# Cross-attention with layer norm: the first transfers split over two queues, a shorter warm-up, and one tile squared before it is centred

## The chip, the cores and the metric

The kernel runs on one core of a Trainium2 chip. The metric is the device time of one execution in microseconds (us). Engines are named as in the profile: PE is TensorE, ACT is ScalarE, DVE is VectorE, POOL is GpSimd, SP is SyncE, which here only issues transfers. PEld is TensorE's loading of weights.

## The reference

Four batches of 2048 queries of width 512 attend to 77 context rows each, with 16 heads of width 32. A residual and a layer norm follow.

```python
qs = (q @ wq).reshape(Bq, Lq, H, HD).transpose(0, 2, 1, 3)
ks_ = (k @ wk).reshape(Bq, Lk, H, HD).transpose(0, 2, 1, 3)
vs = (v @ wv).reshape(Bq, Lk, H, HD).transpose(0, 2, 1, 3)
scores = jnp.einsum('bhqd,bhkd->bhqk', qs, ks_) / jnp.sqrt(jnp.float32(HD))
scores = jnp.where(mask[:, None, :, :], -jnp.inf, scores)
attn_w = jax.nn.softmax(scores, axis=-1)
attn = jnp.einsum('bhqk,bhkd->bhqd', attn_w, vs)
attn = attn.transpose(0, 2, 1, 3).reshape(Bq, Lq, H * HD)
out = attn @ wo + q
mu = jnp.mean(out, axis=-1, keepdims=True)
var = jnp.mean((out - mu) ** 2, axis=-1, keepdims=True)
return (out - mu) / jnp.sqrt(var + EPS) * gamma + beta
```

Here q is x (4 x 2048 x 512), k and v are both the context (4 x 77 x 512), all float32.

## The kernel before, in words

**Tiling.** The 8192 rows are 64 tiles of 128 rows; two tiles are a block, four are a group of 512 rows (`GRP`). A float32 product is made of three products in a rounded format (fp32r): each factor is split into a high part (a cast) and a low part (the rest), and high x high, low x high and high x low are summed. `split(hi, lo, src)` does the cast on ScalarE and the subtraction on VectorE. The width of 512 is cut into four chunks `c` of 128.

**The start.** GpSimd clears a small tile, and TensorE multiplies it by itself: `WARM` large products of 512 columns and then 18 small ones of 32. Their results are not used. Meanwhile the first 256 rows of x, already transposed (`xT0`, two transfers of two chunks each, into `xtf`), and the four chunks of `wq` (into `stage_a`) are loaded, 128 partitions of 2 KB per transfer. One of the six transfers is issued by ScalarE, the others by SP; behind them on SP stand the context (`ctx_f`), `wk`, the mask, the second 256 rows, `wv` and so on. For chunk 0, VectorE casts the weight (`wqh`), ScalarE the input (`xth`), VectorE then makes the low parts `xtl` and `wql`. The 48 products into the four banks `pq` (four chunks, three kinds, four column blocks) follow, and the 48 of the keys behind them (`pk`).

**What sets the order.** Each engine takes its own instructions in the order in which the code issues them. Waits between engines and transfers are set by a tool that follows the tiles. Transfers use eight counters in turn (`DMAHW0` to `DMAHW7`, "lanes" here): the ninth waits until the first has landed. An instruction carries one wait; where it needs more, further waits stand ahead of it as instructions of their own. ScalarE's load of its function table is put ahead of its first computing instruction.

**The middle and the end.** From tile 6 on the order is written out by hand as words in tables (`PAIR`, `JOINT`, `ORDER`): a letter is a step, the number its tile. For the end of the program the words that matter here are

- `I54` (`act_mean`) and `J54` (`act_squares`): ScalarE's mean of the rows of tile 54, and its sum of squares of (row - mean), both from the tile `od[54]`, named `o`;
- `y54` (`centre`): VectorE's (row - mean) x gamma, written back into the same tile;
- `u54` (`rsqrt_one`, GpSimd) and `z54` (`finish`, VectorE): the factor from the sum of squares, and the last step with it and beta;
- `h63.1` and `m63.1`: the reciprocals (VectorE) and the scaling (GpSimd) of the second half of tile 63's weights; `b30.1` and `b30.0`: the low part `AL` of block 30 on VectorE, after ScalarE's `AH`.

Of the kernel before, what the change touches and what calls it, by code (L numbers as in the profile page):

```python
# [17 lines left out]
P = 128  # L18
# [11 lines left out]
NC_D = D // P  # L30
# [2 lines left out]
MASKED = -3.0e38  # L33
CEIL = 2.9e38
EPS = 1.0e-5
WARM = 8
NPB = 3
KSCALE = 1.0 / HD**0.5
LATE = 48
# [19 lines left out]
P27.0s q63 u48 p48 T58.1 T58.2 P26.1s P27.1s P26.11s T58.3 e58.1 r57 t56 P27.11s n57 Q61 P27.6s f46 e58.2 T58.0 V26  # L59
q61 a26.1 t57 a26.0 x55 f48 e58.0 S59 P27.2s T59.2 P27.5s e58.3 T59.3 e59.3 P27.3s P28.4g P27.8s T59.0 O51 b26.0  # L60
P28.11g T59.1 P27.9s +51 P28.6g r58 e59.2 P28.5g O50 P27.10s b26.1 s51 e59.1 P27.4s n58 S60 Y0 u51 +50 P28.0s x57
e59.0 P28.7g P28.10s V27 T60.0 T60.1 a27.0 T60.2 a27.1 T60.3 e60.1 r59 t58 w46 P28.3s P28.9s S61 n59 O52 P28.1s
e60.3 b27.0 s50 T61.0 T61.3 t59 f49 u50 e61.0 e61.3 T61.2 b27.1 T61.1 O53 P28.8s P29.1g P29.9g e61.2 O54 S62 +52
e61.1 +53 s52 x54 r61 P28.2s V28 +54 P29.7g e60.2 x62 T62.1 T62.2 O55 p50 n61 e60.0 T62.3 x56 P29.4s r60 n60 T62.0
t61 v51 M0 P29.8s a28.0 a28.1 b28.1 b28.0 f50 t60 +55 O57 e62.2 P29.6s e62.1 P29.5s P29.10s +57 P30.6g P29.3s
P29.11s k51 P29.2s P29.0s P30.10s P30.1s e62.0 e62.3 u52 v52 S63 V29 P30.2s T63.0 P30.9s P30.5g s53 P30.7g P30.11a
s55 T63.1 r62 a29.1 P30.4s T63.3 P30.0s e63.0 P30.3s n62 b29.1 T63.2 O56 a29.0 b29.0 e63.1 I54 u53 e63.3 P30.8s s57
h63.0 y55 t62 +56 f51 O59 u55 e63.2 x58 O58 x60 k52 m63.0 y54 V30 h63.1 m63.1 I56 U62.7s U62.6s +59 J56 a30.1 u56
U62.4s U62.8s R63.0 U62.9s x61 U62.11s s59 y57 a30.0 u57 +58 u59 b30.1 b30.0 U62.5s z57 R63.1 y53 J54 R63.3 U62.1s
U62.0a R63.2 w48 E63.0a f52 w51 s58 U62.10s O60 U62.3s +60 w50 O61 U62.2a w52 y58 X63 M1 z53 E63.1a v56 v59 s60 z55  # L70
+61 y60 E63.2a u54 W62 u58 k56 E63.3a w49 w57 u60 z54 k59 c62 w54 I61 J61 W63 f56 z58 c63 d62 y61 w53 z60 w55 u61
f59 O62 w56 d63 z61 +62 s62 y62 w58 w61 w59 O63 u62 s63 z62 w60 y63 u63 w62 z63 w63
"""


# [1 line left out]
def xattn_layernorm(  # L77
# [15 lines left out]
    nc = tc.nc  # L93
# [10 lines left out]
    ring, kept, rows, summed = [], set(), {}, set()  # L104
    held = {}

    def bank(name):
        while len(ring) % 8 in kept:
            ring.append(ring[-8])
        ring.append(ring[-8] if kept else ps.tile([P, 512], F32, tag="mm", name=name))  # L110
        return ring[-1]
# [28 lines left out]
    stage_a = sb.tile([P, 2, NC_D, D], F32, tag="PT", name="stage_a")  # L140
# [9 lines left out]
    def wview(w, c):  # L150
        return w[c * P : (c + 1) * P, :]
# [522 lines left out]
    pw = bank("pw")  # L674
    for i in range(WARM):
        nc.tensor.matmul(pw, warm[:, :P], warm[:, None, :P].to_broadcast((P, 4, P)), start=True, stop=True)
    for i in range(18):
        nc.tensor.matmul(pw[:, :32], warm[:, :P], warm[:, :32], start=True, stop=True)

    for c in range(0, NC_D, 2):  # L680
# [2 lines left out]
    qd[0] = sb.tile([P, NG, GRP], F32, tag="q", name="q_0")  # L683
    x0h, x0l = (a[:, :, :BLK] for a in gx[0])
    f0 = {c: fx[0, c].rearrange("p c r -> p (c r)").rearrange("p (h c r) -> p h c r", h=2, c=2) for c in (0, 2)}
    for c in range(0, NC_D, 2):
        nc.sync.dma_start(f0[c][:, 0], xT0[0, :, c : c + 2])
        (nc.sync if c else nc.scalar).dma_start(stage_a[:, 0, c], wview(wq, c))
        nc.sync.dma_start(stage_a[:, 0, c + 1], wview(wq, c + 1))
    for c in range(NC_D):  # L690
        if c % 2 == 0:
            nc.sync.dma_start(ctx_f[:, c : c + 2], ctxT[:, c : c + 2])
# [312 lines left out]
```

## Time and profile before

| | us |
|---|---|
| median of three runs | 507.82 (507.53 to 508.34) |
| the profiled execution, its own time | 506.96 |
| its span in the profile | 505.2 |
| TensorE busy | 496.4 (98%) |
| ScalarE busy | 472.2 (93%) |
| VectorE busy | 463.3 (92%) |
| GpSimd busy | 427.0 (85%) |

The time of an execution is 1.76 us longer than the span, which runs from the first recorded instruction to the last. A row of the timeline has the start, the length, the engine, the line, the operation and what it writes and reads; neighbouring equal instructions are merged with their count, and products overlap, so the length of one is longer than the distance to the next. "SPq" and "ACTq" are the issuing of transfers by SP and ScalarE.

### The profile page before, as it was taken

How to read it: one execution, taken by the hardware profiler on the slowest of the kernel's cores; microseconds unless marked ns; L12 is line 12 of the kernel's file. 1: busy time of each engine (PE TensorE's matmuls, PEld its weight loads, DVE VectorE, ACT ScalarE, POOL GpSimd, SP SyncE). 2: the span in 40 equal slices, each digit the busy share in tenths (PEclk: the TensorE clock that was granted, in tenths of full speed). 3: DMA queues.
4: the chain of work that ended last, by engine and by line, in shares of the span. 5: the costliest groups of instructions: out<-in, count | busy, mean ns of one | idle time of the engine just before them, and what ended most of it. 6: DMA issues, size and time to landing. Idle time of an engine off the chain costs nothing.

```text
span 505.2 us, 20438 instructions
## 1 busy us (share of the span) xinstructions
PE 496.4 (98%) x6908; PEld 391.0 (77%) x6908; DVE 463.3 (92%) x2566; ACT 472.2 (93%) x2239; POOL 427.0 (85%) x384
## 2 busy tenths in 40 slices
PE   9999999999999999999999999999999999999994
PEld 7987778777777887777788777777877777777784
DVE  6698999999989998999999988999999889999997
ACT  6798999999999999999999999999999999999861
POOL 0659368989888998988999888889988888999994
PEclk9999999999999999999999999999999999999999
DMA  8945887677778779777878878787777878667665
GB/s 308 399 165 151 207 215 194 197 191 210 213 226 227 217 211 257 188 205 227 224 218 220 237 182 248 210 228 212 228 200 204 237 214 245 171 189 209 168 210 209
DMA packets 58280, 109.50 MB, mean 217 GB/s; under 512 B 9203, under 2 KB 10739, under 8 KB 58176
## 3 DMA queue, kind: packets, MB, share of 16 engines
q1 hardware_dynamic: 55776, 103.35, 72.5%
q0 software_dynamic: 1872, 4.20, 2.7%
q8 instruction: 55, 0.90, 0.8%
q10 hardware_dynamic: 528, 0.66, 0.4%
q14 instruction: 49, 0.40, 0.2%
HBM read 41.68 MB, written 16.78 MB: 116 GB/s over the span
## 4 chain that ended last, share of the span: by engine, by line
PE 90%; ACT 4%; DVE 3%; DMA 2%; issue 1%; SPq 1%; DVEq 0%; ACTq 0%
PE pq L192 31%; PE po L557 29%; PE pa L459 11%; PE sc L321 7%; PE sc L557 3%; ACT pbuf L379 3%; PE sc_e L321 2%; PE pv L258 2%; PE pk L218 1%; PE pq L709 1%; PE pq L190 1%; DMA PT<-B 1%; PE sc_f L321 1%; DMA xtf<-xT 1%; DVE pbuf L364 1%
## 5 line engine op out<-in xcount | busy, mean ns | idle before, releaser
L379 ACT ACTIVATE pbuf<-pbuf,nm 128x77 f32<-128x77 f32 x1024 | 352.5, 349 | 8.5 <-DVE nm L364 7.5
L379 ACT ACTIVATION_READ_ACCUMULATOR pbuf<-pbuf,nm 128x1 f32 x1024 | 193.5, 189 | 0.0
L390 POOL TENSOR_TENSOR pbuf<-pbuf,ri 128x1232 f32<-128x1232 f32 x63 | 145.9, 2317 | 19.7 <-DVE ri L385 15.7
L364 DVE CUSTOM_DVE_ANT_0 pbuf<-sc,mb 128x77 f32<-128x77 f32 x828 | 144.0, 232 | 5.9 <-PE sc L321 5.6
L192 PE MATMUL pq<-xtl,wqh 128*128 128x512 f32 (+1 forms) x256 | 98.3, 384 | 0.0
L192 PE MATMUL pq<-xth,wql 128*128 128x512 f32 (+1 forms) x256 | 98.2, 384 | 0.0
L413 DVE STREAM_TRANSPOSE B<-pbuf 128x1280 f32<-128x1280 f32 x63 | 94.6, 1503 | 0.4 <-POOL pbuf L390 0.2
L557 PE MATMUL po<-woh,AH 128*128 128x512 f32 x224 | 90.6, 405 | 0.0
L192 PE MATMUL pq<-xth,wqh 128*128 128x512 f32 (+1 forms) x230 | 88.6, 385 | 0.0
L557 PE MATMUL po<-wol,AH 128*128 128x512 f32 x224 | 87.4, 390 | 0.0
L585 POOL TENSOR_TENSOR o<-o,gam 128x512 f32<-128x512 f32 x53 | 68.7, 1297 | 21.0 <-ACT o L581 21.0
L557 PE MATMUL po<-woh,AL 128*128 128x512 f32 x224 | 86.5, 390 | 0.0
L364 DVE DVE_READ_ACCUMULATOR2_ANT nm<- 128x1 f32 x1024 | 84.7, 83 | 0.0
L586 POOL TENSOR_TENSOR o<-o,bet 128x512 f32<-128x512 f32 x53 | 68.4, 1290 | 4.2
L180 POOL TENSOR_TENSOR xtl<-xtf,xth 128x1024 fp32r<-128x1024 f32 x28 | 67.5, 2412 | 0.1
L459 PE MATMUL pa<-PT,vsb 96*32 96x256 f32 x960 | 58.2, 382 | 0.7 <-DMA PT<-B 0.3
L321 PE MATMUL sc<-kct,q 32*64 32x77 f32 x3312 | 55.2, 238 | 0.5 <-DVE q L209 0.5
L192 PEld LDWEIGHTS pq<-xth,wql 128*128 128x128 f32 x256 | 48.2, 188 | 8.4
L192 PEld LDWEIGHTS pq<-xtl,wqh 128*128 128x128 f32 x256 | 48.1, 188 | 8.5
L321 PEld LDWEIGHTS sc<-kct,q 32*64 32x64 f32 x3312 | 48.7, 130 | 6.5 <-issue 4.8
L557 PEld LDWEIGHTS po<-woh,AH 128*128 128x128 f32 x224 | 42.0, 188 | 10.8 <-DVE nm L364 0.4
L192 PEld LDWEIGHTS pq<-xth,wqh 128*128 128x128 f32 x230 | 43.2, 188 | 9.0
(176 smaller groups left out, 851.6 us busy)
## 6 DMA issues: line engine op xcount, KB each, us to landing
PT<-B SPq DMA_DIRECT2D x355, 128.0 KB
xtf<-xT SPq DMA_DIRECT2D x28, 512.0 KB
o<-x SPq DMA_DIRECT2D x56, 256.0 KB
out<-o SPq DMA_DIRECT2D x56, 256.0 KB
PT<-B POOLq DMA_DIRECT2D x16, 128.0 KB, 4.5
o_end<-x SPq DMA_DIRECT2D x7, 256.0 KB
out<-o_end SPq DMA_DIRECT2D x7, 256.0 KB
xtf<-xT SPq DMA_DIRECT2D x4, 256.0 KB
```

Source lines behind the costliest of these rows:

```text
L180: nc.gpsimd.tensor_tensor(l, fx.pop((g, c)), h.bitcast(F32), ALU.subtract)
L192: nc.tensor.matmul(pq, wc, r[:, c, rs], start=(n == 0), stop=(n == 11))
L258: nc.tensor.matmul(pv, ctx_s[c][i][:, r, :], v[c], start=(n == 0), stop=(n == 11))
L321: nc.tensor.matmul(scs[t][g, j][r0 : r0 + n], qd[t // 4][q, g, at : at + n], kct[q, g, t // TPB, keys_of(j)], start=True, stop=True,)
L364: nc.vector.tensor_tensor_reduce(pb[:, i // 2, (i % 2) * NK : (i % 2 + 1) * NK], scs[t][g, j], mb[:, t % TPB, keys_of(h)], -1.0, CEIL, ALU ...
L379: nc.scalar.activation(p, p, AF.Exp, bias=nmax[t][:, i : i + 1], scale=-1.0, accum_out=sums[t][:, i : i + 1])
L390: nc.gpsimd.tensor_tensor(pv, pv, rv.to_broadcast((P, NP, 2, NK)), ALU.mult)
L413: nc.vector.transpose(bt.rearrange("p c q r -> p q c r"), pbuf[t % NPB].rearrange("p q (c r) -> p q c r", c=5),)
L459: nc.tensor.matmul(pas[b, g // 2][HD * j : HD * (j + 1), (g % 2) * BLK : (g % 2 + 1) * BLK], vsb[:, 2 * b // TPB, HD * h : HD * (h + 1)], ...
L557: nc.tensor.matmul(pos[t][:, cols], a[:, c, rs], w[:, c, cols], start=go, stop=done)
L585: nc.gpsimd.tensor_tensor(o, o, gam, ALU.mult)
L586: nc.gpsimd.tensor_tensor(o, o, bet, ALU.add)
```

## The change

Four edits. Two of the eight large warm-up products go, and two small ones are added. The first transfer of x is cut into 96 and 32 partitions, both on SP, with half a chunk of `wq` between them. Chunk 0 of `wq` is cut into two halves of 64 partitions, one issued by ScalarE and one by SP; chunk 1 is cut into two halves too, both issued by ScalarE. And `y54` is moved in the table from ahead of `V30` to behind `J54`, so that the squares of tile 54 are taken from the rows themselves and not from the centred ones.

```diff
-WARM = 8
+WARM = 6
@@ ORDER (the rest of the table has the same words in the same order)
-... s57 h63.0 y55 t62 +56 f51 O59 u55 e63.2 x58 O58 x60 k52 m63.0 y54 V30 h63.1 m63.1 I56 ...
+... s57 h63.0 y55 t62 +56 f51 O59 u55 e63.2 x58 O58 x60 k52 m63.0 V30 h63.1 m63.1 I56 ...
-... b30.1 b30.0 U62.5s z57 R63.1 y53 J54 R63.3 U62.1s ...
+... b30.1 b30.0 U62.5s z57 R63.1 y53 J54 y54 R63.3 U62.1s ...
@@
-    for i in range(18):
+    for i in range(20):
         nc.tensor.matmul(pw[:, :32], warm[:, :P], warm[:, :32], start=True, stop=True)
@@
-    for c in range(0, NC_D, 2):
-        nc.sync.dma_start(f0[c][:, 0], xT0[0, :, c : c + 2])
-        (nc.sync if c else nc.scalar).dma_start(stage_a[:, 0, c], wview(wq, c))
-        nc.sync.dma_start(stage_a[:, 0, c + 1], wview(wq, c + 1))
+    def load_x0(queue, c, rows):
+        queue.dma_start(f0[c][rows, 0], xT0[0, rows, c : c + 2])
+
+    def load_wq(queue, c, rows):
+        queue.dma_start(stage_a[rows, 0, c], wview(wq, c)[rows])
+
+    first, second = slice(0, P // 2), slice(P // 2, P)
+    load_x0(nc.sync, 0, slice(0, 96))
+    load_wq(nc.scalar, 0, first)
+    load_wq(nc.sync, 0, second)
+    load_x0(nc.sync, 0, slice(96, P))
+    load_wq(nc.scalar, 1, first)
+    load_wq(nc.scalar, 1, second)
+    load_x0(nc.sync, 2, slice(0, P))
+    load_wq(nc.sync, 2, slice(0, P))
+    load_wq(nc.sync, 3, slice(0, P))
```

The order of the instructions, with the counters that each waits for. ScalarE's first instructions before:

```order
L688 DMA stage_a<-wq 128x512
L154 ACT_TABLE_LOAD
L154 CAST xth_129<-xtf_0_127 128x256 [waits DMAHW1_49]
L154 CAST xth_129<-xtf_0_127 128x256
L154 CAST wqh<-stage_a 128x512 [waits DMAHW2_49]
```

And now:

```order
L690 DMA stage_a<-wq 64x512 x3
L154 ACT_TABLE_LOAD [waits DMAHW5_49]
L154 CAST xth_129<-xtf_0_127 128x256 [waits DMAHW1_49]
L154 CAST xth_129<-xtf_0_127 128x256
L154 CAST wqh<-stage_a 128x512 [waits DMAHW4_49,DMAHW2_49]
```

ScalarE now issues three transfers instead of one; the first cast needs both pieces of x, and of its two waits the one for the piece of 32 partitions (DMAHW5) stands ahead of the table load.

SP's first transfers before:

```order
L687 DMA xtf_0_127<-xT 128x512
L689 DMA stage_a<-wq 128x512
L687 DMA xtf_2_128<-xT 128x512
L688 DMA stage_a<-wq 128x512
L689 DMA stage_a<-wq 128x512
L692 DMA ctx_f<-ctxT 128x768
L693 DMA stage_a<-wk 128x512
L693 DMA stage_a<-wk 128x512 [waits DMAHW0_49]
```

And now:

```order
L687 DMA xtf_0_127<-xT 96x512
L690 DMA stage_a<-wq 64x512
L687 DMA xtf_0_127<-xT 32x512
L687 DMA xtf_2_128<-xT 128x512
L690 DMA stage_a<-wq 128x512
L690 DMA stage_a<-wq 128x512 [waits DMAHW0_49]
L704 DMA ctx_f<-ctxT 128x768 [waits DMAHW1_49]
L705 DMA stage_a<-wk 128x512 [waits DMAHW2_49]
```

The second piece of x is third on SP, behind 64 rows of `wq`; and since the pieces use up the eight counters earlier, SP waits from its sixth transfer on instead of its eighth.

VectorE near the end, before (`o_54` is tile 54; `o_end` are the tiles from 56 on; the second row is `y54`, the third `h63.1`, the ninth and tenth `b30.1` and `b30.0`):

```order
L560 TENSOR_TENSOR o_end_7996<-sc_62_0_8488,o_end_7996 128x512
L655 SCALAR_TENSOR_TENSOR o_54_8534<-o_54_8534,mvt_54_8778,row_0_8609 128x512
L398 RECIPROCAL ri_63_8791<-sum_63_8668 128x8
L560 TENSOR_TENSOR o_end_7996<-sc_62_1_8489,o_end_7996 128x512
L595 BN_STATS st_59_8874<-o_end_7996 128x6
L601 BN_AGGR mvt_59_8876<-st_59_8874 128x2
L655 SCALAR_TENSOR_TENSOR o_end_7996<-o_end_7996,mvt_57_8789,row_0_8609 128x512
L560 TENSOR_TENSOR o_end_7996<-sc_62_2_8490,o_end_7996 128x512
L512 TENSOR_TENSOR AL_30_8861<-pa_28_0_8539,AH_30_8860 128x512
L512 TENSOR_TENSOR AL_30_8861<-sc_62_3_8491,AH_30_8860 128x512
```

And now, from the two `b30` on:

```order
L512 TENSOR_TENSOR AL_30_8863<-pa_28_0_8542,AH_30_8862 128x512
L512 TENSOR_TENSOR AL_30_8863<-sc_62_3_8494,AH_30_8862 128x512
L664 SCALAR_TENSOR_TENSOR o_end_7999<-o_end_7999,mvt_57_8792,bet_74 128x512
L655 SCALAR_TENSOR_TENSOR o_53_8005<-o_53_8005,mvt_53_8729,row_0_8612 128x512
L655 SCALAR_TENSOR_TENSOR o_54_8537<-o_54_8537,mvt_54_8781,row_0_8612 128x512
L595 BN_STATS st_58_8913<-o_end_7999 128x6
L601 BN_AGGR mvt_58_8915<-st_58_8913 128x2
L560 TENSOR_TENSOR o_end_60_8833<-sc_62_2_8493,o_end_60_8833 128x512
```

The centring of tile 54 has moved ten instructions down on VectorE, behind that of tile 53, and now waits for ScalarE's `J54`; `h63.1` and what stood behind it up to `b30.1` move up by one.

More of the change, by code (lines that the diff above doesn't have):

```diff
@@ L61 @@
 P28.11g T59.1 P27.9s +51 P28.6g r58 e59.2 P28.5g O50 P27.10s b26.1 s51 e59.1 P27.4s n58 S60 Y0 u51 +50 P28.0s x57
[L62 to L70, printed above, removed]
@@ L71 @@
-+61 y60 E63.2a u54 W62 u58 k56 E63.3a w49 w57 u60 z54 k59 c62 w54 I61 J61 W63 f56 z58 c63 d62 y61 w53 z60 w55 u61
-f59 O62 w56 d63 z61 +62 s62 y62 w58 w61 w59 O63 u62 s63 z62 w60 y63 u63 w62 z63 w63
+e59.0 P28.7g P28.10s V27 T60.0 T60.1 a27.0 T60.2 a27.1 T60.3 e60.1 r59 t58 w46 P28.3s P28.9s S61 n59 O52 P28.1s e60.3
+b27.0 s50 T61.0 T61.3 t59 f49 u50 e61.0 e61.3 T61.2 b27.1 T61.1 O53 P28.8s P29.1g P29.9g e61.2 O54 S62 +52 e61.1 +53
+s52 x54 r61 P28.2s V28 +54 P29.7g e60.2 x62 T62.1 T62.2 O55 p50 n61 e60.0 T62.3 x56 P29.4s r60 n60 T62.0 t61 v51 M0
@@ new lines @@
+P29.8s a28.0 a28.1 b28.1 b28.0 f50 t60 +55 O57 e62.2 P29.6s e62.1 P29.5s P29.10s +57 P30.6g P29.3s P29.11s k51 P29.2s
+P29.0s P30.10s P30.1s e62.0 e62.3 u52 v52 S63 V29 P30.2s T63.0 P30.9s P30.5g s53 P30.7g P30.11a s55 T63.1 r62 a29.1
+P30.4s T63.3 P30.0s e63.0 P30.3s n62 b29.1 T63.2 O56 a29.0 b29.0 e63.1 I54 u53 e63.3 P30.8s s57 h63.0 y55 t62 +56 f51
+O59 u55 e63.2 x58 O58 x60 k52 m63.0 V30 h63.1 m63.1 I56 U62.7s U62.6s +59 J56 a30.1 u56 U62.4s U62.8s R63.0 U62.9s x61
+U62.11s s59 y57 a30.0 u57 +58 u59 b30.1 b30.0 U62.5s z57 R63.1 y53 J54 y54 R63.3 U62.1s U62.0a R63.2 w48 E63.0a f52
@@ L73 @@
+w51 s58 U62.10s O60 U62.3s +60 w50 O61 U62.2a w52 y58 X63 M1 z53 E63.1a v56 v59 s60 z55 +61 y60 E63.2a u54 W62 u58 k56
+E63.3a w49 w57 u60 z54 k59 c62 w54 I61 J61 W63 f56 z58 c63 d62 y61 w53 z60 w55 u61 f59 O62 w56 d63 z61 +62 s62 y62 w58
+w61 w59 O63 u62 s63 z62 w60 y63 u63 w62 z63 w63
 """
```

## The prediction

> **What bounds the kernel now.** I read the page's first part, then the chain of work that ended last in order of time over the first 57 us, the timeline of the first 7 us engine by engine, and the timeline of the last 25 us.
>
> ```profile
> span 505.2 us, 20438 instructions
> PE 496.4 (98%) x6908; PEld 391.0 (77%) x6908; DVE 463.3 (92%) x2566; ACT 472.2 (93%) x2239; POOL 427.0 (85%) x384
> PE 90%; ACT 4%; DVE 3%; DMA 2%; issue 1%; SPq 1%; DVEq 0%; ACTq 0%
> ```
>
> TensorE is busy for 98% of the span and makes 90% of the chain, so what counts is when its useful products start, and whether it waits afterwards. The chain (start, length, what) runs from the first input through the first two blocks of products:
>
> ```profile
> 0.73 3.65 DMA xtf<-xT
> 4.38 0.02 issue
> 4.40 0.72 ACT xth L154 x2
> ...
> 5.14 6.04 PE pq L709 x48
> 11.18 7.03 PE pk L218 x48
> ...
> 55.83 0.89 PE sc L321 x53
> 56.72 0.22 DVE pbuf L364
> ...
> 57.04 5.61 ACT pbuf L379 x32
> ```
>
> From 5.14 to 56.7 us it is products end to end; where ScalarE takes over at 57.04, it was started by products of that chain. So a later first product (L709) moves everything behind it, the end too. The waits of TensorE behind the start bound what could be given back:
>
> ```profile
> PE sc L321 <- DVE q L209: 0.5, 1, 0.5
> PE pa L459 <- DMA PT<-B: 0.3, 1, 0.3
> PE pa L459 <- issue: 0.2, 1, 0.2
> ```
>
> The 0.5 us lies inside the stretch that ScalarE sets, which moves along; I take nothing for them.
>
> The first 7 us (start, length, engine, what, and in brackets the idle time before it and what ended it):
>
> ```profile
> 0.73 0.40 SPq L687 DMA_DIRECT2D xtf<-xT  x1
> 1.18 0.42 SPq L689 DMA_DIRECT2D stage_a<-wq  x1
> 1.64 0.43 SPq L687 DMA_DIRECT2D xtf<-xT  x1
> 0.73 0.41 ACTq L688 DMA_DIRECT2D stage_a<-wq  x1
> 1.18 1.28 ACT L154 ACT_TABLE_LOAD   x1 [1.18 <-PEq L996]
> 4.40 0.71 ACT L154 CAST xth<-xtf 128x256 fp32r<-128x256 f32 x2 [1.94 <-DMA xtf<-xT]
> 4.57 0.43 DVE L701 CAST wqh<-stage_a 128x512 fp32r<-128x512 f32 x1 [2.66 <-DMA stage_a<-wq]
> 4.91 0.42 DVE L155 TENSOR_TENSOR xtl<-xtf,xth 128x256 fp32r<-128x256 f32 x1
> 5.25 0.69 DVE L704 TENSOR_TENSOR wql<-stage_a,wqh 128x512 fp32r<-128x512 f32 x1
> 0.93 3.60 PE L676 MATMUL pw<-ident 128*128 128x512 bf16 x8 [0.93 <-POOL ident L667]
> 4.32 0.69 PE L678 MATMUL pw<-ident 128*128 128x32 bf16 x18
> 5.14 0.76 PE L709 MATMUL pq<-xth,wqh 128*128 128x256 f32 x4
> 5.74 0.64 PE L709 MATMUL pq<-xtl,wqh 128*128 128x256 f32 x4
> 6.21 0.64 PE L709 MATMUL pq<-xth,wql 128*128 128x256 f32 x4
> ```
>
> Three things end near 5 us: the input's cast (4.40 plus 0.40), the weight's cast on VectorE (4.57 + 0.43 = 5.00) and the warm-up (4.32 + 0.69 = 5.01). The weight's cast and the warm-up are last, and the first product follows 0.14 later. ScalarE's one function-table load, 1.28 us, is over at 2.46, hidden under the wait for the input.
>
> **The change, part by part.**
>
> *Warm-up.* Eight large products took 4.32 - 0.93 = 3.39 us, 0.424 each; six end at 3.47. Twenty small ones at 0.69/18 each take 0.77, so the warm-up is over at 4.24 instead of 5.01. That frees TensorE 0.77 us earlier, and is worth nothing unless input and weight are earlier too.
>
> *The wait ahead of the table load.* This is the term that decides. The first cast (xth, chunk 0) now needs two transfers, 96 partitions on lane DMAHW1 and 32 on DMAHW5. In the instruction order shown above, the wait for DMAHW5 stands ahead of ACT_TABLE_LOAD, where before that load waited for nothing. ScalarE takes its instructions in order, so the load begins only when the last 32 partitions are there, and the cast comes 1.28 us behind that. What was hidden from 1.18 to 2.46 is then on the path. The other two DMAs that ScalarE now issues (about 0.46 each, until some 2.1 us) are hidden under the same wait.
>
> *When those 32 partitions land.* No row shows it, so I bound it by bytes moved (stretch, then last column GB/s):
>
> ```profile
> 0.50:2.00 1.50, 1.07 (x3) 0.44 (x4) 0.82 (x10) 0.82 (x1) 0.50 (x8) 1.00 0.08 19
> 2.00:4.30 2.30, 2.30 (x6) 0.76 (x5) 0.00 (x0) 0.46 (x1) 0.00 (x0) 1.00 0.79 284
> 4.30:5.10 0.80, 0.71 (x19) 0.58 (x17) 0.53 (x2) 0.70 (x3) 0.00 (x0) 1.00 1.10 410
> ```
>
> Before, 262 KB stood on SP's queue up to the end of the input; now 393 KB do, since 64 rows of weight lie between its two pieces. The extra 131 KB take 0.32 us at 410 GB/s if SP's queue has the engines to itself, and 0.64 if ScalarE's queue, which now holds 393 KB too, takes every second turn. From 4.38 that gives 4.70 to 5.02. As the outer low end I keep 4.38, the landing of before. I take 4.85, the middle of the inner two. The third issue on SP stands at 1.64 to 2.07, far ahead of that, so issuing doesn't set it.
>
> The Trainium skill, "DMA: Bandwidth & Descriptors", section "Rules for kernel authors", advises against two transfers to disjoint halves of the partitions, as both share the same 16 engines and nothing is won. By that rule the landing is the late end, 5.02, and the time 0.17 us above my forecast; the trace has input and weight, on two queues, landing 0.17 us apart (4.40 and 4.57), which agrees with sharing.
>
> *The first product.* 4.85, + 0.02 to the load, + 1.28, + 0.02, + one cast of 0.40 (mean below), + 0.14 from the end of a cast to the first product (5.00 to 5.14): 6.71 against 5.14, **+1.57 us**. Ends: +1.10 with 4.38, +1.74 with 5.02.
>
> ```profile
> L154 ACT CAST xth<-xtf 128x256 fp32r<-128x256 f32 x3 | 1.1, 404 | 2.0 <-DMA xtf<-xT 1.9
> ```
>
> *What follows on VectorE.* Its weight cast needs only the weight (about 4.6, as before) and is out of the way. xtl then starts 0.10 behind the cast (4.91 against 4.81), wql 0.34 later with 0.69: done 1.13 behind the cast's end. TensorE reaches the wql products 1.07 after the first product, 1.21 behind the cast's end. That just fits; 0 to +0.1.
>
> *Clock.* The first four products took 5.74 - 5.14 = 0.60 us, the next four 0.47: TensorE came to full speed only there. If it is at full speed at 6.7, 0.13 us comes back.
>
> *Later loads.* SP's third wq load now waits for DMAHW0, ScalarE's first piece, so it and all loads behind it are issued some 1.5 us later at first (2.59 becomes about 4.2). The engines have the bytes ahead of it to move until nearly 6 us, and the products that need it start 1.57 later as well: 0.
>
> *Tile 54.* Its centring on VectorE leaves 479.36 and comes in behind the one of tile 53, at 485.90. J54 on ScalarE reads the uncentred tile, and needs the same time.
>
> ```profile
> 479.36 0.73 DVE L655 SCALAR_TENSOR_TENSOR o<-o,mvt,row 128x512 f32<-128x512 f32 x1
> 480.01 0.19 DVE L398 RECIPROCAL ri<-sum 128x8 f32<-128x8 f32 x1
> ...
> 483.38 0.69 DVE L512 TENSOR_TENSOR AL<-pa,AH 128x512 fp32r<-128x512 f32 x1 [0.44 <-ACT AH L508]
> ...
> 485.24 0.74 DVE L655 SCALAR_TENSOR_TENSOR o<-o,mvt,row 128x512 f32<-128x512 f32 x1
> 485.90 0.69 DVE L595 BATCH_NORM_STATS2 st<-o_end 128x6 f32<-128x512 f32 x1
> 487.39 0.69 DVE L560 TENSOR_TENSOR o_end<-sc,o_end 128x512 f32<-128x512 f32 x1 [0.58 <-PE sc L557]
> 483.72 0.73 ACT L621 ACTIVATE spare<-o,mvt 128x512 f32<-128x512 f32 x1
> 479.92 2.40 POOL L403 TENSOR_TENSOR pbuf<-pbuf,ri 128x616 f32<-128x616 f32 x2
> ```
>
> The five instructions ahead of 483.38 move up by 0.65 and then wait 1.09 instead of 0.44 there, for the same cast on ScalarE; the reciprocal that moves up feeds the second half of a GpSimd operation that runs without a gap from 479.92, so nobody starts earlier. The new wait, for J54, is over at 484.5, before VectorE comes to it. The 0.65 that is put in at 485.90 eats the 0.58 of idle before 487.39: +0.07 at most, 0 taken.
>
> *Sum.* +1.57 - 0.13 + 0.05 = **+1.5 us**. On the profiled execution, 506.96 us with a span of 505.2, that is 508.5 and 506.7. That execution lies 0.86 below the median of the three runs, 507.82, to which I add the same: **509.3 us**, 0.3% slower.
>
> **The rivals.**
>
> *The clock comes late.* Behind the warm-up's end at 4.24 TensorE would now be idle until 6.7, 2.5 us, and its warm-up is 0.77 us shorter. In the trace full speed came 4.2 to 4.8 us after the first warm-up product, with hardly a gap between. If the gap spoils that, the products at 6.7 run at half speed: 0.212 for 256 columns (half of 0.424) against 0.119 (0.47/4), a loss of 0.44 us for each us of it. Were all of the 4.2 to 4.8 us to be gone through again, that is +2.0: 511.3. With part of it, 510 to 511. For it speaks the gap; against it that most of the warm-up is still there. Chance 0.2. The Trainium skill, "TensorE: Matmul & The Clock Gate", Part 1, says that the clock is released by a window of about 3.4 us of sustained activity whose phase is not tied to the kernel; by it a warm-up of 3.3 us can miss a window in some executions, which is this rival. The trace shows the release once and can't show its phase.
>
> *The load costs more than its 1.28.* Between its end at 2.46 and the cast at 4.40 the row leaves 1.94 us in which a settling time could be hidden. At 4.85 it would show. The Trainium skill, "ScalarE: Activation LUTs", section "What ACT_TABLE_LOAD costs", puts a drain of about 1.4 us behind a load, 2.7 in all. Worked out from the row, half of the 1.94 gives 510.3, all of it 511.2. Against it: the load is the first one, with nothing to drain. Chance 0.08.
>
> *Not slower.* The point on which it turns is whether the table load really runs behind that wait. If it starts at about 2.1, after ScalarE's issues, it is done by 3.4 and hidden as before; then input and weight alone set the start. With a landing from 4.38 to 4.85 the first product comes at 4.94 to 5.4 (cast 0.40, and 0.14): 507.6 to 508.1, no change. For it speaks that the load has no data to wait for; against it the order on ScalarE's queue. A landing so early, near 4.0, that even the exposed load costs only 0.7 ends here too (508.5). Chance 0.17. Faster by 1 us would need a first product at 4.1, ahead of the warm-up's end: 0.02.
>
> **How the numbers follow.** 0.2% is 1.0 us, and about what a measurement of this kernel can tell from no change. The forecast, 508.9 to 509.6, has 0.53; late clock 0.20, dearer load 0.08, not slower 0.17, faster 0.02. The range from 508.4 to 511.3 takes in the forecast, most of the two dearer cases, and the upper end of no change; left out are most of the 0.17, the 0.02 and a tail above. Slower is 0.53 + 0.20 + 0.08 = 0.81, less nothing for the forecast's low end (+1.1 - 0.1 = 1.0), which lies at the bound.
>
> **What would show it.** In the timeline of after: ACT_TABLE_LOAD starting between 4.4 and 5.0 instead of 1.18, released by the transfer into xtf; the first cast 1.3 us behind it; the warm-up over at 4.2 and the first L709 product near 6.7, after more than 2 us of idle; four of them in 0.47 us if the clock is up, in 0.85 if not. At the end, VectorE's idle before its first AL near 1.1 us. I am wrong if the load stays near 2.1, or if TensorE's waits behind the start shrink by as much as the start is late.

## The result, and the profile after

| | before, us | after, us |
|---|---|---|
| median of the comparison, 4 runs each | 507.67 (507.42 to 508.34) | 511.75 (511.01 to 512.26) |
| the profiled execution, its own time | 506.96 | 511.42 |
| its span | 505.2 | 509.3 |

The change makes the kernel slower by 0.8%: the ratio is 1.0077, interval 1.006 to 1.0095. The forecast was 509.3 with an upper end of 511.3; the time lies above it.

The chain of work that ended last (start, length, what), with the first 23 us:

```profile
1.80 4.21 DMA xtf<-xT
...
6.08 0.98 ACT L154
...
7.38 0.41 ACT xth L154
...
7.84 7.76 PE pq L721 x48
15.60 7.03 PE pk L218 x48
```

The first product starts at 7.84 instead of 5.14 (+2.70), and the 48 products then take 7.76 us instead of 6.04 (+1.72). Together that is 4.42 at the first key product (15.60 against 11.18), and it stays: the last writing of an output on VectorE begins at 505.68 against 501.36, +4.32. The span is longer by 4.1; outside it, an execution takes 2.1 us here (511.42 against 509.3) and 1.76 before.

```profile
505.68 0.48 DVE o_end L660
```

The rows of the timeline behind these sums (start, length, engine, what; in brackets the idle time before, and what ended it):

```profile
0.74 1.94 ACTq L690 DMA_DIRECT2D stage_a<-wq  x3
3.47 0.74 PE L678 MATMUL pw<-ident 128*128 128x32 bf16 x20
5.16 0.43 DVE L713 CAST wqh<-stage_a 128x512 fp32r<-128x512 f32 x1 [3.24 <-DMA stage_a<-wq]
6.08 1.28 ACT L154 ACT_TABLE_LOAD   x1 [6.08 <-DMA xtf<-xT]
7.38 0.71 ACT L154 CAST xth<-xtf 128x256 fp32r<-128x256 f32 x2
7.84 1.23 PE L721 MATMUL pq<-xth,wqh 128*128 128x256 f32 x4 [3.63 <-ACT xth L154]
11.42 0.82 PE L721 MATMUL pq<-xtl,wqh 128*128 128x256 f32 x4
12.08 0.64 PE L721 MATMUL pq<-xth,wql 128*128 128x256 f32 x4
```

ScalarE waits for x until 6.08, only then loads its table, and casts at 7.38. TensorE idles for 3.63 us, and its first four products take 1.23 us against 0.76 before; groups of four are back at 0.64 only from 12.08 on. The DMA engines moved this (stretch, then the last column, GB/s):

```profile
2.00:4.30 2.30, 2.21 (x24) 1.08 (x22) 0.00 (x0) 0.00 (x0) 0.00 (x0) 1.00 0.88 241
4.30:5.10 0.80, 0.00 (x0) 0.00 (x0) 0.00 (x0) 0.00 (x0) 0.00 (x0) 1.00 1.00 297
5.10:6.10 1.00, 0.00 (x0) 0.00 (x0) 0.43 (x1) 0.02 (x1) 0.00 (x0) 1.00 0.83 238
```

In the first two stretches it was 284 and 410 before. From 2.0 to 6.0 us that is 554 + 238 + 214, about 1000 KB, although only 786 KB are issued up to the second piece of x, even with all three pieces of ScalarE counted in: more than 200 KB of what SP issues behind it had been moved by then.

The trace also has 16 landing events for each transfer, apart from the rows, and a wait for the transfer ends with the last of them. Those of the 32 partitions come from 4.52 to 6.01; before, those of the whole transfer of x come from 4.00 to 4.38. On SP the 96 partitions are complete at 3.36, the half of `wq` at 5.06 and the 32 partitions at 6.01, on ScalarE the three pieces at 3.92, 6.18 and 7.03. So on each queue the transfers are complete in the order of issue, and what is late of x's second piece is the last of its 16 parts.

### The profile page after: what moved, and what is told of

Same layout as the page of the kernel before. It is cut to its first block, busy times and chain, and to the rows that moved or that the text cites. A ratio compares the mean times of both kernels' runs of the same rounds, so it can differ in the third digit from the quotient of the medians.

```text
span 509.3 us, 20445 instructions
## 1 busy us (share of the span) xinstructions
PE 497.2 (98%) x6908; PEld 392.5 (77%) x6908; DVE 462.6 (91%) x2566; ACT 471.8 (93%) x2239; POOL 428.1 (84%) x384
## 4 chain that ended last, share of the span: by engine, by line
PE 91%; ACT 4%; DVE 2%; DMA 1%; issue 1%; SPq 0%; DVEq 0%; ACTq 0%
PE pq L192 31%; PE po L557 30%; PE pa L459 11%; PE sc L321 7%; PE sc L557 3%; ACT pbuf L379 3%; PE sc_e L321 2%; PE pv L258 2%; PE pq L721 2%; PE pk L218 1%; PE pq L190 1%; PE sc_f L321 1%; DMA xtf<-xT 1%; DMA PT<-B 1%; DVE o_end L655 0%
```

## The experiments

Each kernel computes the whole reference, with other transfers, other warm-up products or another place of one step. `e1` and the like are labels, and "after" is the changed kernel. "Before" is the kernel before in runs on the same chip beside them. The ratio stands near that of the means, so that it can differ from that of the medians where executions fall in groups.

| run | edit | median, us | range | before | ratio, interval |
|---|---|---|---|---|---|
| e1 | the split transfers alone | 511.89 | 511.51 to 512.23 | 507.57 | 1.0088, 1.0073 to 1.0103 |
| e2 | the shorter warm-up alone | 508.95 | 506.62 to 509.57 | 507.57 | 1.0014, 0.9996 to 1.0031 |
| e5 | tile 54 alone | 507.28 | 506.65 to 508.05 | 507.62 | 0.9997, 0.9987 to 1.0007 |
| e3 | after, table load drawn ahead | 510.19 | 509.21 to 512.38 | 507.57 | 1.0069, 1.0045 to 1.0093 |
| e4 | after, warm-up up to the first product | 510.07 | 509.31 to 511.13 | 507.57 | 1.0053, 1.0038 to 1.0068 |
| e6 | both | 509.12 | 508.58 to 515.07 | 507.62 | 1.0053, 1.0026 to 1.008 |
| e7 | e3, pieces by columns | 508.68 | 507.32 to 509.99 | 507.62 | 1.0025, 1.0012 to 1.0037 |
| e8 | e3, x ahead of wq's second half | 511.09 | 508.47 to 512.36 | 507.62 | 1.0061, 1.0034 to 1.0088 |
| e10 | only x cut by rows | 509.37 | 508.27 to 510.89 | 507.43 | 1.0046, 1.003 to 1.0062 |
| e11 | only wq's chunk 0 cut by rows | 508.31 | 507.46 to 509.17 | 507.43 | 1.0016, 1.0004 to 1.0027 |
| e16 | only wq's chunk 0 cut by columns | 508.25 | 506.56 to 512.98 | 507.29 | 1.0018, 0.999 to 1.0046 |
| e15 | e3, chunk 1 of wq whole on SP | 508.66 | 507.72 to 509.57 | 507.29 | 1.0031, 1.0019 to 1.0044 |
| e12 | e7 with the warm-up of before | 508.48 | 507.55 to 509.81 | 507.43 | 1.0025, 1.0015 to 1.0034 |
| e9 | before, warm-up 6 large and 42 small | 515.63 | 514.78 to 516.26 | 507.43 | 1.0172, 1.0156 to 1.0187 |
| e13 | before, 6 large and 20 small, wider | 507.23 | 506.59 to 508.13 | 507.29 | 1.0, 0.999 to 1.0009 |
| e14 | before, same length in 48 products | 514.83 | 514.7 to 516.84 | 507.29 | 1.016, 1.0141 to 1.0179 |

**Which part of the change.** Three kernels do one part each: before with the new transfers and warm-up and table of before (e1); before with `WARM = 6` and `range(20)` (e2); before with the new table of words (e5).

> The old warm-up (8 large, 18 small) and the old tail, with only the transfers split. Theory (the wait ahead of the table load, a later landing, and a slow clock caused by TensorE's idle time behind its warm-up): table load at about 6.0 us, first product at 7.8, half speed for a part of the first 48 products because the gap from 5.0 to 7.8 is still there; 1.0 to 1.7 us lost by that, so +3.7 to +4.4 us, 511.3 to 512.1. Rival (the clock is late because the warm-up is shorter): first product at 7.8 too, but the 48 products take 6.0 as before; +2.7, 510.4. Rival (the splitting costs little by itself): +1 at most.

> Only the warm-up changed (6 large, 20 small), transfers and tail as before. Theory: TensorE is idle from 4.2 to 5.1 us, too short a gap to matter much; first product at 5.14 as before, 0 to +0.4 us. Rival (the shorter warm-up makes the clock late): the 48 products take 7.5 us or more instead of 6.0; +1.5 us, 509.2.

> Only tile 54's centring moved behind its squares; transfers and warm-up as before. Theory: the start is untouched, VectorE's wait ahead of its first AL grows from 0.44 to about 1.1 us and the end moves by 0.1 at most; 507.5 to 507.8, no change. Rival (the move delays VectorE's last chain): up to +0.65, 508.2.

The transfers alone make the whole difference (511.89), and tile 54 makes none. The chain of e1:

```profile
1.80 4.00 DMA xtf<-xT
...
5.87 0.99 ACT L154
...
7.62 7.50 PE pq L721 x48
```

With the long warm-up the products are nearly as slow (7.50) as with the short one (7.76), so the shorter warm-up alone is not what makes them slow; TensorE idles for 2.6 us ahead of them in this run, and the clock record below shows what that does. The short warm-up by itself is not free either. Its ten executions fall in two groups, 506.62 to 507.13 (four) and 508.85 to 509.57 (six), nothing between, about 2.4 us apart. The profiled one is of the lower group:

```profile
5.07 5.98 PE pq L709 x48
```

**How much is the table load, how much the clock.** e3 puts a two-column copy on ScalarE behind its three issues, so that the load comes at 2.70; e4 keeps TensorE busy until the first product; e6 does both (110 small products).

```diff
+    nc.scalar.copy(small[:, 40:42], mhalf)     # e3, e6: behind the first transfers
-    for i in range(20):
+    for i in range(150):                       # e4; 110 in e6
         nc.tensor.matmul(pw[:, :32], warm[:, :P], warm[:, :32], start=True, stop=True)
```

> The changed kernel with a two-column copy on ScalarE behind its three transfers, so that the function table is loaded at about 2.7 to 4.0 us, ahead of the wait for x. Theory: 1.28 us come back at the first product (7.84 becomes 6.5), and perhaps a little at the clock; -1.3 to -2.0 against the changed kernel, 509.7 to 510.5. Rival (the table load isn't on the path, the landing alone is): no change, 511.7.

> The changed kernel with 150 small warm-up products instead of 20, which keep TensorE busy until about 7.6 us. Theory: first product at 7.84 as in the changed kernel, but at full speed from the start; the 48 products take 5.8 to 6.0 us instead of 7.76, -1.7 to -1.9, 509.8 to 510.1. Rival (the slow clock is a matter of chance and has nothing to do with the gap): 48 products between 6.0 and 7.8 as the run has it, 510 to 511.7, no closer together than the changed kernel's runs (511.0 to 512.3).

> The changed kernel with the table load ahead of the wait and 110 small warm-up products, busy until about 6.4 us. What is left of the split is the later landing of x alone. Theory: x lands at 5.6 to 6.0, first product at 6.1 to 6.5, the 48 products take about 6.0; 1.0 to 1.4 us slower than before, 508.6 to 509.0. Rival (landing without effect once the other two are gone): 507.6.

Chain of e3, then e4:

```profile
1.81 3.73 DMA xtf<-xT
...
5.62 0.41 ACT xth L154
...
6.08 7.28 PE pq L722 x48
```

```profile
7.79 6.12 PE pq L721 x48
```

With the load drawn ahead the cast follows x at once, and 1.6 us of the 4.1 come back (511.75 to 510.19; in the trace x also lands 0.47 us earlier than in after, so that not all of it need be the load's); with TensorE kept busy the 48 products take 6.12 instead of 7.76 from the same late start, and 1.7 come back (three of its four executions lie below all of the changed kernel). Both together bring 2.6, not 3.2, and leave e6 just above the expected 508.6 to 509.0. In e6 the key products, not the first, are what is late, because the transfer of `wk` is:

```profile
5.83 5.51 DMA stage_a<-wk
...
12.77 7.01 PE pk L218 x46
```

**When the pieces land.** Even with both repairs 1.5 us are lost. e7 cuts the same pieces by columns, over all 128 partitions (x 384 and 128 columns, wq 256 and 256); e8 issues x's second piece ahead of wq's second half on SP.

Excerpts of both edits:

```diff
-    load_x0(nc.sync, 0, slice(0, 96))          # e7: rows of partitions
+    load_x0(nc.sync, slice(0, 384))            #     columns of all partitions
-    load_wq(nc.sync, 0, second)                # e8: the one moved
     load_x0(nc.sync, 0, slice(96, P))
+    load_wq(nc.sync, 0, second)
```

> As the kernel with the table load first, but every piece is cut by columns and covers all 128 partitions: x in 384 and 128 columns, wq chunks 0 and 1 in halves of 256 columns; same queues, same order, same bytes in each piece. If part-partition pieces are what makes the landing late, the last piece of x lands at about 4.9 and wq chunk 0 at 4.6. If the place behind other bytes on two busy queues does it, x lands at 5.5 to 6.0 as before. First cast needs only the first piece here and may come at 3.5 to 4.4.

> As the kernel with the table load first, but the 32 partitions of x are issued ahead of the second half of wq chunk 0, so both pieces of x are first on SP. If the place in SP's queue makes the landing late, x lands at 4.0 to 4.4 and the second half of wq last, at about 5.0 or later; first product 5.5 or later. If part-partition pieces do it, x lands at 5 or later in spite of its place.

Two rows of e7's timeline, then two of e8's chain and one of its timeline:

```profile
4.51 0.43 DVE L717 CAST wqh<-stage_a 128x512 fp32r<-128x512 f32 x1 [2.60 <-DMA stage_a<-wq]
4.96 0.41 ACT L154 CAST xth<-xtf 128x256 fp32r<-128x256 f32 x1 [0.73 <-DMA xtf<-xT]
```

```profile
1.64 4.23 DMA stage_a<-wq
...
6.55 8.31 PE pq L722 x48
```

```profile
4.20 0.71 ACT L154 CAST xth<-xtf 128x256 fp32r<-128x256 f32 x2
```

Same queues, order and bytes: by columns the piece that stands third on SP is there at 4.9, by rows at 5.5 (e3; its first landing events are as early, 4.29 against 4.37, its last are not), and when wq's half stands third, that half comes at 5.9 (e8), while x was cast at 4.20. So the late one is the row piece that stands third. (e8's time is worse than e3's because its 48 products take 8.31 us: full speed comes at 11.82. By columns, chunk 0 of x also lies wholly in the first piece, so that its cast waits for one transfer.)

Four more kernels take the cuts one by one: e10 and e11 cut only x or only wq's chunk 0 in the kernel before; e16 is e11 by columns; e15 is e3 without the two further transfers on ScalarE. Excerpts:

```diff
+        for part in (slice(0, 96), slice(96, P)) if c == 0 else (slice(0, P),):     # e10
+            nc.sync.dma_start(f0[c][part, 0], xT0[0, part, c : c + 2])
-    load_wq(nc.scalar, 1, first)                                                    # e15
-    load_wq(nc.scalar, 1, second)
+    load_wq(nc.sync, 1, slice(0, P))
```

> Before, with only the first transfer of x cut into 96 and 32 partitions, which SP issues one behind the other; wq whole, one transfer on ScalarE, warm-up 8 and 18. The table load is behind the second piece again. Theory A (a piece of part of the partitions lands late by itself): the 32 partitions land at 5.3 or later, table load there, first product near 7.1, 48 products at half speed in part: 510.5 to 512. Theory B (pieces land late only where three cut transfers of wq stand beside them, since the bytes ahead and the issuing are more): the 32 partitions land at 4.4 to 4.6, first product 6.3 to 6.5: 508.8 to 510.5, by the clock.

> Before, with only chunk 0 of wq cut into two halves of 64 partitions, the first issued by ScalarE, the second by SP behind x, which is whole. One transfer is waited for ahead of the first cast of x, so the table load is hidden (1.2 to 2.5). Theory A (a piece of part of the partitions lands late by itself): the second half lands at 5.3 or later, weight cast there, first product near 6.0, 0.8 later than before: 508.2 to 510.5. Theory B (it was late for the three cut transfers beside it): second half at 4.5 to 4.7, first product 5.1 to 5.3: 507.3 to 508.0, no difference from before.

> The changed kernel with the table load drawn ahead by a tiny copy, and chunk 1 of wq whole on SP behind the last piece of x, instead of two halves on ScalarE: ScalarE issues a single piece of 128 KB. Compare with the same kernel with both halves on ScalarE (last piece of x at 5.6, first product 6.08, 510.2). Theory A (ScalarE's further transfers are drawn ahead of x's last piece): it lands at 4.7 to 5.0, first product 5.3 to 5.6, 508.0 to 509.5. Theory B (row pieces on both queues are enough): 5.4 or later, first product 5.9 to 6.2, 509.5 to 510.5.

> Before, with chunk 0 of wq alone cut into two halves by columns (all 128 partitions, 1 KB each) on ScalarE and SP, where the same cut by rows of partitions gave 508.3 with the second half at about 4.8 and wq's chunk 1 at 6.3. Theory A (row pieces are slower to land): halves at 4.4 to 4.6, first product at 5.1, 507.3 to 507.8. Theory B (by rows or by columns is the same, the extra transfer is what counts): as by rows, 508.1 to 508.6.

Rows of e10 (chain), e11 (chain), e15 (timeline) and e16 (timeline):

```profile
1.18 3.67 DMA xtf<-xT
...
4.92 1.28 ACT L154
```

```profile
1.17 3.57 DMA stage_a<-wq
```

```profile
5.21 0.71 ACT L154 CAST xth<-xtf 128x256 fp32r<-128x256 f32 x2 [2.35 <-DMA xtf<-xT]
```

```profile
4.42 0.43 DVE L702 CAST wqh<-stage_a 128x512 fp32r<-128x512 f32 x1 [2.51 <-DMA stage_a<-wq]
```

Cut alone, x is there at 4.85 (whole: 4.38), between the two theories and nearer to the one without lateness of its own; with half a chunk of wq between its pieces, and one piece on ScalarE, at 5.12 (e15, cast at 5.21); with three pieces on ScalarE at 5.5 to 6.0 (e3, e1, e4, after). Read from one trace each, the cut costs about 0.5, the half between and the piece on ScalarE 0.3, and ScalarE's 256 KB further 0.4 to 0.9. e15's landing so lies between its two theories, its time in theory A. e11's half comes at 4.74, just behind theory B's range, but its time is theory A's. By columns (e16) the cast starts 0.4 earlier, 4.42 against 4.84. But the time of e16 is that of e11: theory A held for the landing and theory B for the time. The second half of the products waits in e16 for wq's third chunk, cast at 8.91; the same is seen in e15, at 8.60. (In e16's trace the landing events of whole transfers are far apart too, from 5.74 to 8.02 for x's chunks 2 and 3, so late last parts are not confined to row pieces.) The rows of e16:

```profile
2.59 6.30 DMA stage_a<-wq
...
8.91 0.63 ACT wqh L154
...
9.58 3.14 PE pq L710 x24
```

**The best of it.** e12 takes e7 and the warm-up of before.

> The changed kernel with three repairs: the pieces cut by columns over all 128 partitions instead of by partitions, ScalarE's table load drawn ahead by a tiny copy behind its three issues, and the warm-up of before (8 large and 18 small products). Theory A (late pieces, exposed load and idle time ahead of the first product were the whole loss): first product at 5.0 to 5.2, the 48 products in about 6.0, 507.4 +- 0.4, no execution in the group above 508.5, no difference from before (507.6). Rival (two queues cost something besides): 508 to 509 as the same without the long warm-up, 508.7.

The first product is at 5.04, 0.10 ahead of before, and yet the median is 508.48, 0.25% (0.15 to 0.34) above before; the rival held. Its chain runs through the loads behind:

```profile
3.98 0.33 SPq L693
...
4.36 0.44 SPq L708
...
4.84 5.47 DMA stage_a<-wk
...
10.98 0.70 DVE wol L155
...
11.73 7.02 PE pk L218 x46
```

SP's last transfer of wq (L693) stands in a wait for a landed piece until 3.98, since the pieces have used up the eight counters, and the context and `wk` behind it are issued that much later: at 4.36 and 4.84, where before had them at 3.06 and 3.54 in its timeline. `wk` lands at 10.31 and the key products begin at 11.73 against 11.18. Of the 1.05 us, 0.3 lies outside the span: the time is 2.11 us longer than the span in e12 (median of twelve executions) and 1.80 in before. All kernels with three transfers on ScalarE have 1.9 to 2.1 there, all others 1.8; no row shows why. No version tried with split transfers beats the kernel before.

**What the clock asks for.** e9 takes two large products away but closes the gap with small ones.

> Before, with the two large warm-up products gone (6 instead of 8) but 42 small ones instead of 18, so that the warm-up still ends near 5.0 and there is no idle time ahead of the first product. Nothing else is changed. Theory A (what costs in the shortened warm-up is the 0.9 us of idle time ahead of the first product, since a stretch of the clock's watch is then not full): as before, 507.6 +- 0.4, every execution under 508.3, 48 products in about 6.0 us. Theory B (large products count for the clock and small ones don't, or less): two groups of executions as with the shortened warm-up alone, near 506.9 and near 509.3, with the upper one in about 6 of 10.

Neither theory: 515.63, 8 us slower, with a start like that of before (key products at 11.45 against 11.18). The loss is in the middle. A row of its timeline, and the waits of TensorE in e14 (total, times, longest), where the number of products is all that was to differ:

```profile
107.93 0.22 PE L321 MATMUL sc_f<-kct,q 32*64 32x77 f32 x1 [1.26 <-issue]
```

```profile
PE sc_e L321 <- issue: 5.4, 4, 1.5
PE sc_f L321 <- issue: 2.4, 3, 0.9
```

TensorE stops in the middle of a row of score products, waiting for nothing that the profile shows, 7.8 us in all in seven places; before has no such line for these products (the last section comes back to these stops). Two kernels then part length from number: e13 keeps 26 products (6 large, 20 of 84 columns instead of 32), e14 replaces the 8 large by 30 of 128 columns.

```diff
+    for i in range(20):                                                                       # e13
+        nc.tensor.matmul(pw[:, :84], warm[:, :P], warm[:, :84], start=True, stop=True)
+    for i in range(30):                                                                       # e14
+        nc.tensor.matmul(pw[:, :128], warm[:, :P], warm[:, :P], start=True, stop=True)
```

> Before, with 6 large warm-up products instead of 8, and 20 small ones of 84 columns instead of 18 of 32: 26 instructions as before, and the warm-up again ends near 5.0, with no idle time. Theory A (the idle time is what costs): as before, 507.5 +- 0.5, nearly all executions under 508.5, 48 products in 6.0 to 6.4 us. Theory B (the length of the large products counts, not the gap): two groups as with the shortened warm-up alone, near 506.9 and near 509.3, median above 508.5. In both no stall of TensorE at the scores for instructions.

> Before, with the 8 large warm-up products of 512 columns replaced by 30 of 128 columns, so that the warm-up lasts about as long but has 48 instructions instead of 26, as in the bridged warm-up of 6 and 42. Theory A (the number of TensorE's instructions ahead sets where its supply of instructions breaks off, and falls into the rows of small score products): 513 to 516, with waits named issue of 1.2 to 1.6 us ahead of score products about every third block. Theory B (the number is indifferent, something else in that run cost the 8 us): 507 to 508.

Both by theory A. Two rows of e13's timeline:

```profile
3.47 1.22 PE L678 MATMUL pw<-ident 128*128 128x84 bf16 x20
5.14 0.71 PE L709 MATMUL pq<-xth,wqh 128*128 128x256 f32 x4 [0.45 <-ACT xth L154]
```

The warm-up ended at 4.69, not at 5.0 as meant, and 0.45 us of idle time cost nothing in any of ten executions (all under 508.2). In e2, with 0.88 us behind a warm-up that ends 0.5 us earlier, six of ten lost 2.4 us. So the two large products themselves, at equal length, are worth nothing. e14 has a start like that of before (first product at 5.18, 48 in 5.99) and 514.83.

What the clock did is on record: each trace keeps, apart from the rows, the clock that TensorE was granted. Full speed is recorded in before from 5.25 us on, in e4 from 6.89, in e2's profiled execution from 3.91, but in after only from 11.82, with nothing ahead of it. (The third last column of the stretches in the section on the result, the granted clock, reads 1.00 there all the same: it takes off recorded losses alone.) In e1 the clock is full from 4.73, half from 8.15 to 11.56, and then full again. Up to the end of the program each of these records lasts a whole number of stretches of 3.413 us. Reckoned back in such stretches, the first full speed stands in all 18 traces at the end of the first stretch in which TensorE idled for 0.63 us or less; stretches with 0.79 or more brought none.

In after the stretches begin at 1.58, 4.99 and 8.41. The warm-up ends at 4.20 and leaves 0.79 us of the first one idle, the wait for x takes 2.84 us of the second, and only the third is filled. In e1 the longer warm-up fills a stretch, and the clock is lost again behind the next one, with 2.63 us of idle time; 1.47 us (e15) did not lose it. Where the stretches begin differs from execution to execution, though every warm-up starts at 0.93. For e2's, from 0.93 to 4.20, a stretch must begin between 0.30 and 1.42 to have 0.63 us of idle time or less. That is a third of the 3.413 us, an estimate from these figures, and near the four of ten in e2's lower group; of the upper six no trace is kept.

## Why the prediction was wrong

**Direction and place were right.** The loss is in the first 16 us, the table load starts behind the transfer into `xtf` and takes 1.28, ScalarE's other issues are hidden, and nothing behind gives it back.

**When those 32 partitions land** is the term that was mis-sized: 4.85 forecast, 5.02 as the late end, 6.01 measured, +1.2 us. It was worked out from bytes in the order of issue, at the rates of before. Two assumptions fell. The rates sank (241 and 297 GB/s for 284 and 410), and the bytes are not moved one transfer after the other: about 1000 KB had been moved for the 786 counted, and the wait is for the last of 16 landing events, 1.5 us behind the first. Without ScalarE's two further pieces x lands at 5.12 (e15), with them at 5.53 (e3). The outer bound was drawn below (4.38) but not above; an upper one from all that could go ahead was missing. The Trainium skill, "DMA: Bandwidth & Descriptors", section "Rules for kernel authors", which the prediction weighed, says that transfers to disjoint halves of the partitions gain nothing and that one transfer over 128 partitions is to be used. The runs agree, and show that they lose: 4.4 whole, 4.85 cut once, 5.5 to 6.0 with all cuts.

**The first product** came at 7.84 against 6.71. The way from the landing on was as forecast: 1.28 for the load, 0.41 for the cast, and 0.06 rather than 0.14 from the cast to the product. In the medians, drawing the load ahead is worth 1.6 us (e3). The rival *The load costs more than its 1.28* is out: the load ends at 7.36 and the cast starts at 7.38, so nothing has to settle behind this load. *Not slower* is out too, since the load did run behind that wait.

**Clock.** The forecast counted +0.13 in favour, and held the late clock as a separate case at 0.2. It came: +1.72, inside the 2.0 put down for that rival. So the case of 0.2 was the one that happened, but with a landing beyond the bound the sum passed its 511.3 all the same. The step that failed is to treat idle time as a side case, with a warm-up that was still thought long enough. In after's trace the warm-up left 0.79 us of its stretch idle and brought no full speed at all; the first came at 11.82. In e1, where the longer warm-up did bring it, 2.6 us of idle time lost it again. The Trainium skill, "TensorE: Matmul & The Clock Gate", Part 1, describes a free-running window of about 3.4 us, so that the transition depends on where the first products fall in it. The clock records agree, with stretches of 3.413 us, and they show the phase, of which the prediction said that the trace can't show it. That is one execution of each kernel: the two groups of e2, and e10's 508.27 to 510.89, fit, but of their longer times no trace is kept. Filling the gap takes the loss away in e4, and halving it in e13.

**Warm-up: worth nothing alone.** Right for the profiled kind of execution (506.62), wrong for six of ten (+2.4): the idle time it leaves was not priced.

**What follows on VectorE; Later loads.** In the changed kernel both cost nothing that shows, as forecast (0.05 and 0). The 0 for the later loads held only because the first products were so late: as soon as the start is repaired, the loads are the bound (e6 12.77, e12 11.73, e15 and e16 in the middle of the products). The cover was named as the products starting later, and when it goes, 0.5 us and more appear.

**Tile 54.** Right: no effect in e5, and in the rows of after the waits that were forecast:

```profile
484.07 0.20 DVE L398 RECIPROCAL ri<-sum 128x8 f32<-128x8 f32 x1 [0.25 <-ACT pbuf L379]
487.70 0.69 DVE L512 TENSOR_TENSOR AL<-pa,AH 128x512 fp32r<-128x512 f32 x1 [0.70 <-ACT AH L508]
489.56 1.40 DVE L655 SCALAR_TENSOR_TENSOR o<-o,mvt,row 128x512 f32<-128x512 f32 x2
```

0.25 and 0.70 instead of the 1.09 in one place; the two centrings stand together in the last row. (Six instructions move up ahead of the `AL`, not five, as the rows of before show; nothing hangs on it.)

**Sum.** +1.5 forecast at the first key product, +4.42 measured: 1.2 from the landing, 1.8 from the clock, less 0.1 at the hand-over and on VectorE. e4 takes the clock's part away, e3 the table load that was forecast, e6 both, and e7 the load and the late landing. What stays open: why the last parts of a cut by partitions land later than those of one by columns, by which rule the two queues share the engines, and what takes 0.3 us outside the span.

## What to carry to other kernels

Here the cut of a first load was paid three times: by the wait for the last piece (ahead of a table load, if that is the first thing behind the wait), by the idle time in which the clock is lost, and, once the start is repaired, by counters that later loads lack; look at all three before adding up bytes. If a first load has to be cut, try columns before partitions, though neither won here; draw ScalarE's table load ahead with an instruction that needs no data, and let the warm-up run up to the first product. If the number of TensorE's instructions ahead of a tuned stretch changes, look there for waits named issue before blaming what was changed.

## What the runs showed of the hardware that was not expected

- Twenty-two products more in the warm-up, at the same length, cost 7.5 us far behind it (e14, 514.83 against 507.29; e9 likewise). The seven stops of 0.6 to 1.5 us, about 45 us apart, lie in the rows of small score products, in which TensorE takes instructions fastest, 0.01 us apart. Ninety and 130 more did not show it (e6, e4; e4 is 260 instructions more, with the weight loads). That it is the supply of instructions which stops is seen in the traces. The page of e14's profile has a queue for it:

```profile
q8 instruction: 55, 0.90, 0.8%
```

Its packets are of 16 KB, 55 for TensorE's 14,146 instructions, about one for every 257. Counted with weight loads and semaphore instructions, the seven stops stand ahead of the instructions 3009, 4289, 5569 and so on to 10689, always five times 256 apart, in e14 and in e9 alike, and each ends 1.2 to 1.6 us behind the end of a packet. Without the stop, the 256 instructions ahead would have taken 2.0 to 2.3 us; the fastest such block of before takes 2.6. So the 44 instructions more have moved the blocks until one holds the fastest stretch alone. The Trainium skill, "Runtime: NRT & Kernel Launch", section "Instruction fetch mechanics", has the instructions streamed in blocks of 256, and their loading mostly hidden; a shift of 260 would then be nearly none and one of 44 a real one, which agrees, but in these two runs the loading is not hidden.
- Issuing a piece of 64 partitions takes 0.57 to 0.68 us on either queue (0.57 in after, the row at 1.19), and the transfer behind one on SP takes 0.57 to 0.63 (after, e8, e11, e15), against 0.42 before (the row at 1.18). That both engines issue at once is not the reason: with three transfers on ScalarE, but cut by columns, SP's take 0.40 to 0.43 (e7, e12).
- A wait for the last of several transfers can turn into a wait ahead of the table load: 1.28 us that a tiny copy hides (e3).
- Of ten executions of one kernel with 0.88 us of idle time ahead of its first products, four took 506.6 to 507.1 and six 508.9 to 509.6; with 0.45 us, none was in the upper group.
- In 18 traces TensorE's full speed came at the end of the first stretch of 3.413 us in which it idled for 0.63 us or less; 0.79 us was too much (after, e8). Once there, it outlasted 1.47 us of idle time in a stretch (e15) and not 2.63 (e1).
